# A fifth buffer of exponentials in an attention encoder, shared with the scaled rows of a part

## The chip, the cores and the metric

The kernel runs on one NeuronCore of one Trainium2 chip. The metric is the device time of one execution in microseconds (us): the median of three runs. Profiled times are counted from the start of the profiled span. The engines are called TensorE (PE), VectorE (DVE), ScalarE (ACT), GpSimd (POOL) and SyncE (SP, which only starts transfers).

## The reference

Four graph layers over N = 2708 nodes with 512 features, each followed by a residual and a layer norm. Only layer 0 is touched, and of it only the encoder. There, H = 4 heads of D = 128 features are weighted by a masked softmax over the adjacency matrix:

```python
Xw = einsum('hnd,hde->hne', Xh, W)
f1 = einsum('hnd,hd->hn', Xw, V[:, 0, :, 0])
f2 = einsum('hnd,hd->hn', Xw, V[:, 1, :, 0])
sig = sigmoid(f1[:, :, None] + f2[:, None, :])
local_att = masked_softmax(adj * sig, adj != 0)      # att is the mean of two equal ones
Xa = einsum('hij,hjd->hid', att, Xw)                  # encoder
Xn = batchnorm(Xa as N x 512)
...                                                   # an MLP block, then the decoder
Y = einsum('hij,hjd->hid', att, Yh)                   # the same att once more
```

So for each head a 2708 x 2708 matrix of exponentials is formed and multiplied with Xw; the sums of its rows divide the result. The decoder, the MLP and layers 1 to 3 follow.

## The kernel before, in words

**Parts and places.** The encoder is the first call of `attention_pass` (`first` is true). The 2708 destination nodes are cut into two halves of 1354 (`HSPAN`), the four heads into two pairs (`HP` = 2). Half by pair gives four parts, in this order: A1 (first half, first pair), B1 (first half, second pair), A2 and B2. In a part the 22 blocks of source nodes are taken in the order of `ORDER`; the position in it is called a place, 0 to 21. Place 11 is the last block, with only 20 nodes.

**One place.** `form` makes the exponentials of one block for both heads in one tile `t` of 128 x 2708 numbers: two tanh on ACT (L403, one for each head; the sigmoid written through tanh), one `scalar_tensor_tensor` on DVE (L411, "the masking step" below, for both heads), one exp on ACT (L412). In the A parts the adjacency block itself is prepared before, by two DVE steps (L391, L392), and stored for later passes; the B parts load the prepared block. PE then multiplies: `node_sums` issues for each head 11 products (10 of 128 destination nodes and one of 74), L433, that add up over the 22 places in four PSUM tiles for each head. Three of these tiles (tags po0 to po2) have a bank for each of the two heads; two more tiles hold the fourth bank of each.

**Buffers.** The tiles `t` come from a pool with four buffers (L479), so a tanh that writes a new tile waits until the tile four places before has been read by everything. The readers of a tile are PE and, in some places, a transfer on POOL's queue (L493, `kept`) that saves it in DRAM for the decoder: at places 8, 11, 14 and 18 in A parts and at places 1, 4, 7, 9, 11, 14, 17 and 20 in B parts (`KEPT`).

**The end of a part.** `keep` empties the eight banks on DVE: for each group of banks the sums are clamped (L634), inverted (L635) and multiplied with the results (L636) into the tile `rows` of that head (L623, a tag of its own with two buffers: one tile for each head). Each bank has to be emptied before the next part's first products can write it. Then `turn` transposes `rows` on PE (L653, 11 for each head, and one more for the sums, L661) into banks of the second head, and DVE copies these into `ft` (L673) and takes their statistics (L675). `turn` of the first head is called at place 0 of the next part, after the first head's products, and `turn` of the second head at place 1. The second head's products of places 0 and 1 come after that. The scaled tile of the row sums also goes to DRAM for the decoder.

**f1b.** Each part needs two tiles with the values of f1 of its heads, spread over the partitions, from three buffers. The first is loaded by SP ahead of time; the second (L464, started from ACT's queue) takes the buffer that the old part's first-head tanh of place 21 reads last.

**What sets the order.** A tile framework orders the instructions of each engine when the program is built, and each engine then runs its own list strictly in that list's order, waiting on semaphores. Which buffer a tile gets follows the order in which the tiles are asked for, the oldest one first. So a change in the buffers also changes the built lists. In the built list of ACT before, in A parts, the first-head tanh of a place stands directly ahead of the exp of two places before; in B parts ACT works in pairs of places.

Of the kernel before, what the change touches and what calls it, by code (L numbers as in the profile page):

```python
# [8 lines left out]
F32 = mybir.dt.float32  # L9
# [8 lines left out]
P = 128  # L18
# [11 lines left out]
def gnn_stack_kernel(  # L30
# [107 lines left out]
    NHALF, HB, HP = 2, 3, 2  # L138
    HW = 2 * ((N + 3) // 4)
# [12 lines left out]
    NB = len(NODES[0])  # L152
# [31 lines left out]
    with ExitStack() as l0:  # L184
# [143 lines left out]
        def spread_sums(att, hf, p):  # L328
# [6 lines left out]
                )  # L335
            return t

        def attention_pass(values, first, att, psum, finish, f1b=None, blocks=(), spread=None, rest=None, taken={}):


# [106 lines left out]
            for hf, (h0, w) in enumerate(HSPAN):  # L447
                for p in range(H // HP):
# [24 lines left out]
                    for place, jt in enumerate(ORDER):  # L473
                        n = BLOCKS[jt][1]


                        if place > (3 if first else 0) and later:
                            later.pop(0)()
                        t = att.tile([P, HP, HW], F32, tag="t", name="t", bufs=4)  # L479
                        tv = t[:n, :, :w]  # L480
                        kept = kept_d.get((hf, p, jt))
                        if kept is None or first:
                            rows = n if n == P else HR
                            with ExitStack() as order:

                                for ins in taken.values() if place == 2 else ():
                                    order.enter_context(tc.issue_after(ins.ins))
                                step = form(hf, p, jt, att, prepare, f1b, t[:rows, :, :w])
                            if rest is not None:
                                rest(step)  # L490
                                rest = None
                            if kept is not None:
                                nc.gpsimd.dma_start(kept[:n, :, :w], tv)  # L493
                        else:
                            for r in range(0, P if n == P else HB * Q, P if n == P else Q):
                                nc.sync.dma_start(t[r : r + n, :, :w], kept[:n, :, :w])
                            if p == 0 and jt in KEPT[1]:
                                count(hf, jt, att)
                        if po is None:


                            both = [
                                psum.tile([P, HP, BANK], F32, tag=f"po{q}", name="po", bufs=1)
                                for q in range(HB)
                            ]
                            po = [both[q][:, k, :] for k in range(HP) for q in range(HB)]
                            if first:
                                more = [
                                    psum.tile([P, BANK], F32, tag=f"psm{k}", name="po", bufs=1)
                                    for k in range(HP)  # L510
                                ]
                                po = [
                                    [both[q][:, k, :] for q in range(HB)] + [more[k]]
                                    for k in range(HP)
                                ]
                        if first:
                            node_sums(0, place, jt, t, w, hf)
                            waiting.append(lambda a=(1, place, jt, t, w, hf): node_sums(*a))
                            if turns:
                                turns.pop(0)()  # L520
                            if not turns:
                                for work in waiting:
                                    work()
                                waiting = []
                            continue
                        for k in range(HP):
                            h = HP * p + k
                            for q, (q0, qw) in enumerate(HCH[hf]):
                                r = 0 if n == P else q * Q
                                nc.tensor.matmul(  # L530
                                    po[HB * k + q][:, :qw],
                                    values[r : r + n, jt, h * P : (h + 1) * P],
                                    t[r : r + n, k, q0 : q0 + qw],
                                    start=(place == 0),
                                    stop=(place == NT - 1),
                                )
# [69 lines left out]
        with (  # L606
# [8 lines left out]
            def keep(hf, p, po, later):  # L615
                h0, w = HSPAN[hf]
                if hf == 0 and p == 0:
                    mlp_w.append(load_mlp(enc_wT, "enc_w"))
                kept = []
                for k in range(HP):  # L620
                    rc = att.tile([P, NB], F32, tag="rc", name="rc", bufs=4)
                    nc.vector.memset(rc[:, NB - 1 :], 1.0)
                    rows = att.tile([P, NB, P], F32, tag="rows", name="rows")  # L623
                    groups = []
                    for b in range(HB + 1):
                        own = list(range(b * PER, min(NB, (b + 1) * PER)))
                        whole = [r for r in own if NODES[hf][r][1] == P]
                        groups += [(b, g) for g in (whole, [r for r in own if r not in whole]) if g]
                    for b, g in groups:
                        m = NODES[hf][g[0]][1]  # L630
                        src = po[k][b][:m, g[0] % PER * DR : (g[-1] % PER + 1) * DR]
                        src = src.rearrange("p (r e) -> p r e", e=DR)
                        own = rc[:m, g[0] : g[-1] + 1]
                        nc.vector.tensor_scalar(own, src[:, :, P], TINY, None, ALU.max)  # L634
                        nc.vector.reciprocal(own, own)  # L635
                        taken[k] = nc.vector.tensor_tensor(  # L636
                            rows[:m, g[0] : g[-1] + 1, :],
                            src[:, :, :P],
                            own.unsqueeze(2).to_broadcast([m, len(g), P]),
                            ALU.mult,  # L640
                        )
                    kept.append((rows, rc))

                def turn(k):

                    h = HP * p + k
                    rows, rc = kept[k]
                    for b in range(TURNS):
                        slots = range(b * QUAD, min(NB, (b + 1) * QUAD))
                        bank = po[1][(TURNS * k + b) % (HB + 1)]  # L650
                        for r in slots:
                            i0, m = NODES[hf][r]
                            nc.tensor.transpose(  # L653
                                bank[:, r % QUAD * P : r % QUAD * P + m],
                                rows[:m, r, :],
                                ident[:m, :m],
                            )
                        c0 = b * BANK
                        cw = min(w, c0 + BANK) - c0
                        if b + 1 == TURNS:  # L660
                            nc.tensor.transpose(bank[:NB, BANK - P :], rc, ident)  # L661
                            sm = att.tile([NB, P], F32, tag="sm", name="sm")
                            nc.vector.tensor_copy(sm, bank[:NB, BANK - P :])
                            full = (NB - 1) * P
                            nc.gpsimd.dma_start(
                                rs_d[h, h0 : h0 + full].rearrange("(r i) -> r i", i=P),
                                sm[: NB - 1],
                            )
                            nc.gpsimd.dma_start(
                                rs_d[h : h + 1, h0 + full : h0 + w], sm[NB - 1 :, : w - full]  # L670
                            )
                        dst = ft[:, h, h0 + c0 : h0 + c0 + cw]
                        nc.vector.tensor_copy(dst, bank[:, :cw])  # L673
                        later.append(
                            lambda dst=dst, n=TURNS * hf + b: nc.vector.bn_stats(  # L675
                                stats[:, h, n, :], dst
                            )
                        )

                return [lambda k=k: turn(k) for k in range(HP)]  # L680
# [1380 lines left out]
```

## Time and profile before

| what | value |
|---|---|
| median of 3 runs | 3207.96 us (3207.13 to 3212.84) |
| the profiled execution | 3204.93 us, of which the span is 3203.1 us |
| encoder pass, first to last L433 on PE | 39.0 to 543.5 us |
| PE busy in it, by part (ends at 168.05, 290.70, 424.00, 543.50) | 114.7, 113.4, 117.6, 110.1 us |
| length of the parts | 129.05, 122.65, 133.30, 119.50 us |
| DVE busy by part | 116.1, 81.7, 124.1, 74.4 us |
| ACT busy by part | 110.0, 111.4, 110.3, 102.3 us |

The parts are cut where PE ends the products of place 21. Busy times of matmuls overlap a little, so PE's share is somewhat high. A line of the timeline has the start, the length, the engine, the line of the kernel and the operation, output and inputs, the shape and how many instructions were merged; in brackets stands how long the engine had been idle before and what ended the wait. PE's records come two for each product, so 44 records are one place of two heads.

### The profile page before, as it was taken

Reading aid. Unit: us, or ns where it says so; the run is one execution under the profiler, and the core shown is the slowest. Engines: PE = TensorE matmul, PEld = TensorE weight load, DVE = VectorE, ACT = ScalarE, POOL = GpSimd, SP = SyncE. Lnnn points to the kernel's source line nnn. Section 1 sums busy time; section 2 is a strip of 40 time slices with the busy share of each in tenths; the row PEclk is TensorE's granted clock in tenths of the full one; section 3 lists DMA queues with packets and bytes.
Section 4 is the critical chain, followed back from the end, with each engine's and each line's share of the span. In section 5 each row is a group of like instructions: output and inputs, shape, how many; then the busy total and the mean of one; then the engine's idle time right before and its main releaser. Section 6 shows DMA issues by size and latency. Waiting matters only on the chain.

```text
span 3203.1 us, 39602 instructions
## 1 busy us (share of the span) xinstructions
PE 3107.7 (97%) x15176; PEld 2353.6 (73%) x15176; DVE 2052.1 (64%) x3797; ACT 1350.0 (42%) x1615; POOL 203.6 (6%) x304
## 2 busy tenths in 40 slices
PE   8888899999999999999999999999999999999999
PEld 7888888454444446885578787777668888888886
DVE  7867975777587585445157766777644555555565
ACT  6898887567777552001133333434401111111111
POOL 1100100000000000000011111110110000000000
PEclk9999999999999999999999999999999999999999
DMA  7866764336545512551054444555431111111111
GB/s 278 297 206 218 280 244 158 109 122 254 177 160 200 184 61 84 144 134 47 30 152 128 148 147 145 157 172 176 133 107 36 49 51 51 49 49 53 49 44 34
DMA packets 203635, 425.81 MB, mean 133 GB/s; under 512 B 20798, under 2 KB 134562, under 8 KB 197622
## 3 DMA queue, kind: packets, MB, share of 16 engines
q1 hardware_dynamic: 179454, 319.92, 33.0%
q0 software_dynamic: 23552, 101.26, 8.4%
q8 instruction: 119, 1.95, 0.2%
q10 hardware_dynamic: 440, 2.10, 0.2%
q14 instruction: 70, 0.57, 0.1%
HBM read 325.88 MB, written 95.87 MB: 132 GB/s over the span
## 4 chain that ended last, share of the span: by engine, by line
PE 72%; issue 11%; DVE 7%; DMA 5%; ACT 3%; POOL 1%; SPq 0%; DVEq 0%; POOLq 0%; ACTq 0%
PE po L1537 18%; PE ps_s L1333 17%; PE po L530 10%; PE ps_nb L1147 7%; PE ps_wide L1197 5%; PE ps_hid L131 2%; PE ps_sup L1725 2%; PE ps_mlp L783 2%; PE po L433 2%; PE ps_dec L914 2%; PE ps_v L131 1%; ACT t L412 1%; DVE t L411 1%; ACT t L403 1%; DMA kept<-t 1%
## 5 line engine op out<-in xcount | busy, mean ns | idle before, releaser
L411 DVE SCALAR_TENSOR_TENSOR t<-t,a 128x2708 f32<-128x2708 f32 (+1 forms) x152 | 450.8, 2976 | 194.8 <-ACT t L403 189.7
L433 PE MATMUL po<-xw,t 128*128 128x129 f32 (+2 forms) x3872 | 448.5, 282 | 48.7 <-ACT t L412 39.0
L433 PEld LDWEIGHTS po<-xw,t 128*128 128x128 f32 (+2 forms) x3872 | 438.1, 192 | 59.2 <-ACT t L412 50.1
L403 ACT ACTIVATE t<-f1b,f2h 128x1354 f32<-128x1354 f32 (+1 forms) x304 | 415.3, 1412 | 74.6 <-PE po L530 33.1
L412 ACT ACTIVATE t<-t 128x2708 f32<-128x2708 f32 (+1 forms) x152 | 371.3, 2452 | 85.5 <-DVE t L411 85.1
L1333 PE MATMUL ps_s<-q,hT 128*128 128x256 f32 (+1 forms) x1848 | 405.5, 372 | 0.0
L530 PE MATMUL po<-t,emb 128*128 128x452 f32 (+3 forms) x1056 | 397.7, 545 | 3.9 <-ACT t L412 3.7
L1537 PE MATMUL po<-sup,e 128*128 128x256 f32 (+1 forms) x1512 | 397.3, 384 | 3.1 <-DVE c L1618 2.1
L1333 PEld LDWEIGHTS ps_s<-q,hT 128*128 128x128 f32 x1848 | 339.2, 190 | 49.8 <-issue 6.0
L530 PEld LDWEIGHTS po<-t,emb 128*128 128x128 f32 (+1 forms) x1056 | 193.5, 190 | 201.1 <-issue 190.8
L1537 PEld LDWEIGHTS po<-sup,e 128*128 128x128 f32 (+1 forms) x1512 | 264.3, 185 | 59.1 <-issue 21.9
L1537 PE MATMUL po<-held,T 128*128 128x256 f32 x1200 | 294.5, 380 | 4.7 <-DVE T L1494 4.7
L1537 PEld LDWEIGHTS po<-held,T 128*128 128x128 f32 x1200 | 226.4, 190 | 38.5 <-DVE T L1494 7.1
L1913 DVE SCALAR_TENSOR_TENSOR e<-a_cols,ps_s 128x512 f32<-128x512 f32 (+1 forms) x121 | 80.0, 661 | 237.9 <-PE ps_s L1333 232.0
L1333 PE MATMUL ps_s<-hT 128*128 128x256 f32 (+2 forms) x968 | 213.9, 372 | 3.4 <-DVE e L1823 2.4
L1333 PEld LDWEIGHTS ps_s<-hT 128*128 128x128 f32 x968 | 174.2, 190 | 30.6 <-issue 3.1
L1819 ACT ACTIVATE a_score<-a_score,neg_big 128x512 f32<-128x512 f32 (+2 forms) x131 | 88.8, 686 | 253.5 <-DMA a_score<-in_adjT_dram 109.5
L1147 PE MATMUL ps_nb<-hid_hi,at 128*128 128x512 f32 x484 | 185.6, 390 | 0.4 <-DVE at L1139 0.4
L1147 PE MATMUL ps_nb<-hid_lo,at 128*128 128x512 f32 x462 | 180.1, 390 | 0.0
L1443 ACT ACTIVATE e<-e 128x512 f32<-128x512 f32 (+1 forms) x187 | 113.5, 617 | 131.4 <-DVE e L1442 131.1
L1494 DVE TENSOR_TENSOR T<-e 128x256 f32<-128x256 f32 x200 | 84.5, 423 | 122.1 <-PE po L1537 98.3
L1905 ACT ACTIVATE q<-ps_wide,uq 128x256 f32<-128x256 f32 (+1 forms) x44 | 20.5, 466 | 336.9 <-PE ps_wide L1197 336.9
(275 smaller groups left out, 3945.7 us busy)
## 6 DMA issues: line engine op xcount, KB each, us to landing
a<-adj_d SPq DMA_DIRECT2D x108, 677.0 KB
a_cols<-in_adjT_dram SPq DMA_DIRECT2D x200, 256.0 KB
a<-in_adjT_dram SPq DMA_DIRECT2D x42, 677.0 KB
adj_d<-a POOLq DMA_DIRECT2D x42, 677.0 KB, 5.8
kept<-t POOLq DMA_DIRECT2D x20, 1354.0 KB, 7.3
t<-kept SPq DMA_DIRECT2D x20, 1354.0 KB
raw<-in_adjT_dram SPq DMA_DIRECT2D x105, 256.0 KB
a_score<-in_adjT_dram SPq DMA_DIRECT2D x55, 256.0 KB
```

What stands on the lines that cost most here:

```text
L131: nc.tensor.matmul(ps[:n], xt[:, c, :n], w[:, c, :], start=(c == 0), stop=(c == C - 1))
L403: tanh = nc.scalar.activation(tv[:, k, :], f1b[k][:n, :w], AF.Tanh, bias=f2h[:n, jt, h : h + 1], scale=0.5,)
L411: step = nc.vector.scalar_tensor_tensor(tv, tv, GUARD, ab, ALU.add, ALU.mult)
L412: exp = nc.scalar.activation(tv, tv, AF.Exp, scale=0.5)
L433: nc.tensor.matmul(po[k][b][:m, s * DR : (s + 1) * DR], t[own : own + n, k, i0 : i0 + m], values[own : own + n, jt, HP * pair + k, :], sta ...
L530: nc.tensor.matmul(po[HB * k + q][:, :qw], values[r : r + n, jt, h * P : (h + 1) * P], t[r : r + n, k, q0 : q0 + qw], start=(place == 0), ...
L1147: nc.tensor.matmul(pos[it][:n], at, half[:, jt, :], start=(jt == 0 and k == 0), stop=(jt == NT - 1),)
L1197: nc.tensor.matmul(ps[:, :width], w(c, o), xt(c), start=(c == 0), stop=(c == C - 1),)
L1333: nc.tensor.matmul(ps[:, jb, i:w], keys[:, c, j : j + P], st["q"][:, c, i:], start=(c == 0), stop=(c == C - 1),)
L1443: nc.scalar.activation(e, e, AF.Exp)
L1537: nc.tensor.matmul(po[bank][rows, half, :], lhsT, rhs, start=(k == 0 and half == 0) if first is None else first, stop=last, skip_group_che ...
L1819: nc.scalar.activation(a, a, AF.Identity, bias=neg_big[: a.shape[0]], scale=1.0e30)
```

## The change

A tile of exponentials in the encoder is now cut out of a slightly larger tile (128 x 2816 instead of 128 x 2708 numbers) of the same tag, which has five buffers. The scaled rows of both heads of a part, 2 x 11 x 128 numbers, are one such tile too, instead of two tiles with a tag of their own. So five buffers hold exponentials, and one of the five holds the scaled rows from the moment a part ends until they have been transposed. The decoder's pass keeps its own four buffers.

```diff
+        def wide_tile(att, name):
+            return att.tile([P, HP * NB * P], F32, tag="t", name=name, bufs=5)
+
...
-                        t = att.tile([P, HP, HW], F32, tag="t", name="t", bufs=4)
+                        if first:
+                            t = wide_tile(att, "t")[:, : HP * HW].rearrange(
+                                "p (k w) -> p k w", k=HP
+                            )
+                        else:
+                            t = att.tile([P, HP, HW], F32, tag="t", name="t", bufs=4)
...
                 kept = []
+                all_rows = wide_tile(att, "rows").rearrange("p (k r d) -> p k r d", k=HP, d=P)
                 for k in range(HP):
                     rc = att.tile([P, NB], F32, tag="rc", name="rc", bufs=4)
                     nc.vector.memset(rc[:, NB - 1 :], 1.0)
-                    rows = att.tile([P, NB, P], F32, tag="rows", name="rows")
+                    rows = all_rows[:, k]
```

Lines after the change are 3 to 9 higher: L403, L411, L412, L433, L634, L636 and L673 become L406, L414, L415, L436, L643, L645 and L682.

## The prediction

> **What bounds the kernel now.** I first read the costliest groups (line, engine, operation, count | busy, mean ns | idle ahead of them and what ended it):
>
> ```profile
> L411 DVE SCALAR_TENSOR_TENSOR t<-t,a 128x2708 f32<-128x2708 f32 (+1 forms) x152 | 450.8, 2976 | 194.8 <-ACT t L403 189.7
> L433 PE MATMUL po<-xw,t 128*128 128x129 f32 (+2 forms) x3872 | 448.5, 282 | 48.7 <-ACT t L412 39.0
> L412 ACT ACTIVATE t<-t 128x2708 f32<-128x2708 f32 (+1 forms) x152 | 371.3, 2452 | 85.5 <-DVE t L411 85.1
> ```
>
> The idle time of L433 is what matters: 48.7 us in the encoder, 39.0 of it for the exp. The other idle times say little, since by stage the bound differs. A place costs PE 39.41/8 = 4.93 us (eight unbroken places from 179.46, below). It costs ACT 4.98 in B parts (two places from 191.00 to 200.96) and DVE 5.49 in A parts (103.65 to 109.14: L391 0.86, L392 1.57, L411 2.98, small gaps). So A parts are bound by DVE; in B parts ACT and PE are level. Next the waits of ACT inside the encoder (total us, times, longest):
>
> ```profile
> ACT t L403 <- DMA kept<-t: 25.2, 9, 5.7
> ACT t L412 <- DVE t L411: 25.0, 16, 6.2
> ACT t L403 <- PE po L433: 10.5, 11, 2.6
> ```
>
> The `kept` transfers hold buffers, and a tanh waits. ACT's timeline in A1 shows how that reaches PE:
>
> ```profile
> 87.23 2.46 ACT L412 ACTIVATE t<-t 128x2708 f32<-128x2708 f32 x1 [0.18 <-DVE t L411]
> 95.44 1.43 ACT L403 ACTIVATE t<-f1b,f2h 128x1354 f32<-128x1354 f32 x1 [5.74 <-DMA kept<-t]
> 96.77 2.44 ACT L412 ACTIVATE t<-t 128x2708 f32<-128x2708 f32 x1
> ```
>
> The exp of place 10 (96.77) had its input at 92.69, but stood behind the tanh of place 12, which waited for place 8's transfer. PE then idled 4.35 us. Last, PE's timeline around A1's end and in B1:
>
> ```profile
> 162.87 5.62 PE L433 MATMUL po<-xw,t 128*128 128x129 f32 x48 [1.88 <-ACT t L412]
> 169.45 0.94 PE L433 MATMUL po<-xw,t 128*128 128x129 f32 x6 [0.97 <-DVE rows L636]
> ...
> 173.61 0.94 PE L433 MATMUL po<-xw,t 128*128 128x129 f32 x6 [1.67 <-DVE rows L636]
> ...
> 175.63 2.72 PE L433 MATMUL po<-xw,t 128*128 128x129 f32 x22 [0.69 <-ACT t L412]
> ...
> 179.46 39.41 PE L433 MATMUL po<-xw,t 128*128 128x129 f32 x352
> 221.02 1.16 PE L433 MATMUL po<-xw,t 128*128 128x129 f32 x8 [2.14 <-ACT t L412]
> ```
>
> and DVE's there:
>
> ```profile
> 170.07 0.13 DVE L634 TENSOR_SCALAR rc<-po 128x1 f32<-128x1 f32 x1
> 170.12 2.97 DVE L411 SCALAR_TENSOR_TENSOR t<-t,a 128x2708 f32<-128x2708 f32 x1
> 173.00 0.55 DVE L636 TENSOR_TENSOR rows<-po,rc 128x384 f32<-128x384 f32 x1
> ```
>
> PE ended place 21 at 168.04 and lost only 0.97 + 1.67 + 0.69 = 3.33 us there, since the masking step of B1's place 0 (160.50 to 163.48) and its exp were done before the emptying. The step at 170.12 is place 1's.
>
> **What the skill says.** "TensorE: Matmul & The Clock Gate", section "Architectural detail: the array is 16× 32×32, not 1× 128×128", says that ACT's and DVE's queues are strictly first in, first out. The trace agrees: the exp above sat 4.1 us behind a waiting tanh. The same page, "What's actually happening", has PE's clock fall to half after an idle window of about 3.4 us, the windows running freely. The trace agrees in kind: from 135.3 to 138.7 the granted clock was 0.51, after only 2.09 us of idleness, and 0.99 in the next 3.4 us. "Perfetto Trace Analysis", "Optimization Strategy", says that regular bubbles can mean that there is no room for a next tile. Only part of the bubbles here are of that kind, as the next steps show.
>
> **The change, step by step.** No instruction comes, goes or changes its size. What changes is which tile waits for which, and with it the built lists of the encoder. All sums are against the profiled execution, 3204.93 us (span 3203.1 and 1.8 around it), 3.0 below the median of 3207.96.
>
> (1) A parts, kept waits: 0. With five buffers a tanh of place p needs place p−5's buffer. But the built list also moves tanh one place ahead: place 13's now stands ahead of the exp of place 10, where place 12's stood. 13−5 = 8 as 12−4 = 8: the exp waits for the same transfer. So PE's gaps in A1 (4.35, 1.51, 2.09) and A2 (3.03, 1.51, 2.42) stay.
>
> (2) B parts, kept waits: −12.0. From place 7 on ACT's list has the old order, so each tanh needs a buffer one place older, now that of a place without a transfer or one finished a place longer. PE's gaps for the exp in B1 (2.14, 0.80, 0.74, 2.22 = 5.90) and B2 (2.96, 2.32, 0.78 = 6.06) go.
>
> (3) Ends of A1 and A2: −2.8. In the list before, the exp of place 21 stands behind the new part's second-head tanh, which waited 3.84 us for f1b. Now all three last exps stand ahead of the new part's six tanh. PE's gaps of 1.88 (at 162.87) and 0.90 (at 418.79) go, and no more, as PE had place 20 to do until 160.99.
>
> (4) A1 to B1 and A2 to B2: +7.2 each, +14.4. The scaled rows need a wide buffer, and the new part's place 0 gets a later place in DVE's list: its masking step moves behind the emptying, to where place 1's stood, and places 1 and 2 move back in turn. By the lines above that position comes 170.12 − 168.04 = 2.08 us after PE's end. Then masking 2.97, exp 2.46 and some 0.1 of hand-over: PE idles 7.6 us where it lost 0.97. Place 1's second-head products then wait for the transposed banks to be copied (L673), with the first head's copies queued behind place 2's masking step and the second head's behind place 3's: I take 1.4 + 1.6 us, estimates, being half a masking step each, with both ends 0 and 3.0. Together 10.6 for 3.33. What was hidden under PE's place 21 is thus uncovered.
>
> (5) B1 to A2: +2.5. The same move; PE started 3.58 us after its end at 290.70, now 7.6: +4.0. A2 is bound by DVE, which loses the 2.98 us that it used to spend on the masking step under PE's tail. If DVE has waits later to swallow it, +1; at most +4.
>
> (6) PE's clock: 0, between −3 and +5. Cold windows of 3.4 us cost PE half of their length, 1.7. Those at 234.3 and 275.3 follow gaps that go; three bubbles of 7.6 us bring up to three, of which B1 to A2 already has one (295.8 to 299.2).
>
> (7) The rest: 0. `ft`, the stored sums, the second pass's loads and the MLP keep their order; the 108 more numbers per tile are never touched.
>
> Sum: −12.0 − 2.8 + 14.4 + 2.5 = +2.1, so 3207.0 for a profiled execution and 3210 for the median.
>
> **Rivals.**
> (a) The bubble stays hidden: 3193. If PE loses no more at the boundaries than before, (4) and (5) vanish and −14.8 remains. For it: five buffers of exponentials, so tanh can be done early. Against it: tanh is not late there, the masking step's place in DVE's list is. It decides if PE's idleness after place 21 is under 3.3 us. Should the kept waits of A parts vanish too, 4.35 + 2.09 + 3.03 + 2.42 = 11.9 more would go; the built list speaks against that.
> (b) The gaps in B parts come back as a shortage at ACT: 3222. ACT's place, 4.98, is not shorter than PE's 4.93, so ACT can't build a lead in a B part; it lives from what it has at the start. After step (4) I estimate, from these rates and the new list, the exp of place 9 some 53 us and PE's need of it some 55 us after the first masking step: a margin of about 2 us. If waits for buffers or for DVE's `ft` copies use it up, PE waits per place again and (2) is lost: +2.1 + 12.0 = +14.
> (c) No effect beyond noise: the likeliest case. The gains of (2) and (3), 14.8, and the losses of (4) and (5), 16.9, are of one size, each uncertain by 3 to 4: −4 to +8 around 3208, thus 3204 to 3216.
>
> **How the numbers follow.** Likeliest case 0.57, (a) 0.15, (b) 0.28. A measurement of this kernel can tell about 0.2%, 6.4 us, from no change. Of the likeliest case 0.52 lie within that and 0.05 above; (b) is mostly above, (a) below. Faster 0.15, same 0.53, slower 0.32. The range reaches into (a) and up to (b): 3197 to 3222. The likeliest alone has 3204 to 3216, its centre being 3210.
>
> **What the profile after would show.** (1) right: ACT's wait for `kept` of 5 to 6 us near 95 is still there. (2): no PE gap over 0.5 us for the exp between the tenth place of B1 and its end. (3): no gap of 1.9 us ahead of place 21. (4), (5): three PE gaps of about 7.6 us for the exp after 166, 288 and 415 or so, with place 0's masking step on DVE in the midst of the emptying. (6): the number of windows at half clock in the encoder, nine before. The prediction is wrong if these gaps are near 3, or if B parts again show gaps of 2 us for the exp.

## The result, and the profile after

The changed kernel takes 3198.3 us (median of 10 runs, 3193.77 to 3204.67); the kernel before, run beside it, 3207.92 (10 runs). The ratio is 0.9971, 95% interval 0.9960 to 0.9982: faster by 0.29%, where +2 us was forecast. The profiled executions are closer: spans of 3196.2 and 3203.1. One execution of either kernel can lie 4 us and more from its median, so what follows compares parts of the encoder, and not spans.

The groups after the change, columns as before:

```profile
L436 PE MATMUL po<-xw,t 128*128 128x129 f32 (+2 forms) x3872 | 444.2, 281 | 43.7 <-ACT t L415 42.6
L415 ACT ACTIVATE t<-t 128x2708 f32<-128x2708 f32 (+1 forms) x152 | 371.7, 2453 | 96.7 <-DVE t L414 96.3
```

PE's idle time in the products fell from 48.7 to 43.7 us only; but 42.6 of it now comes from the exp. The waits of ACT in the encoder:

```profile
ACT t L415 <- DVE t L414: 36.2, 24, 3.8
...
ACT t L406 <- DMA kept<-t: 11.8, 6, 3.2
ACT t L406 <- PE po L662: 5.8, 3, 2.4
ACT t L406 <- PE po L436: 2.5, 2, 1.8
```

The waits for saved tiles fell from 25.2 to 11.8 us, and those for PE's products from 10.5 to 2.5. New are 5.8 us of waits for the transposes (L662), which let go of the shared buffer. Of the 11.8 us all but 1.2, at the end of B1, are in A parts. ACT's timeline in A1:

```profile
94.14 1.42 ACT L406 ACTIVATE t<-f1b,f2h 128x1354 f32<-128x1354 f32 x1 [2.35 <-DMA kept<-t]
95.47 2.44 ACT L415 ACTIVATE t<-t 128x2708 f32<-128x2708 f32 x1
```

This is the exp of place 10 again, behind a tanh (now of place 13) that waits for place 8's transfer, as the prediction had it. PE's timeline, from A1 to the start of A2:

```profile
97.97 10.40 PE L436 MATMUL po<-xw,t 128*128 128x129 f32 x88 [3.58 <-ACT t L415]
...
132.06 29.86 PE L436 MATMUL po<-xw,t 128*128 128x129 f32 x264 [0.64 <-ACT t L415]
169.50 5.10 PE L436 MATMUL po<-xw,t 128*128 128x129 f32 x22 [7.59 <-ACT t L415]
174.40 1.88 PE L662 MATMUL po<-ident,rows 128*128 128x128 f32 x11
...
176.33 2.69 PE L436 MATMUL po<-xw,t 128*128 128x129 f32 x22
...
267.07 14.99 PE L436 MATMUL po<-xw,t 128*128 128x129 f32 x132 [0.60 <-ACT t L415]
289.65 5.10 PE L436 MATMUL po<-xw,t 128*128 128x129 f32 x22 [7.59 <-ACT t L415]
```

and DVE's behind A1's end at 161.91:

```profile
163.94 0.13 DVE L643 TENSOR_SCALAR rc<-po 128x1 f32<-128x1 f32 x1
163.99 2.97 DVE L414 SCALAR_TENSOR_TENSOR t<-t,a 128x2708 f32<-128x2708 f32 x1
166.88 0.55 DVE L645 TENSOR_TENSOR rows<-po,rc 128x384 f32<-128x384 f32 x1
...
171.07 2.97 DVE L414 SCALAR_TENSOR_TENSOR t<-t,a 128x2708 f32<-128x2708 f32 x1
175.49 1.29 DVE L682 COPY ft<-po 128x512 f32<-128x512 f32 x2 [1.46 <-PE po L662]
...
177.90 2.95 DVE L414 SCALAR_TENSOR_TENSOR t<-t,a 128x2708 f32<-128x2708 f32 x1
180.78 1.27 DVE L682 COPY ft<-po 128x512 f32<-128x512 f32 x2
```

So the bubble is there: the masking step begins 2.08 us after PE's end, and with masking and exp PE idles 7.59 us at each of the three boundaries (the third ends at 422.54). The wait that was forecast behind it, for the copies (L682), is not: after 169.50 PE works without a gap until 266. In B1 one gap of 0.60 for the exp is left where there were four of 5.90 in all; in B2 none.

**An account by part.** I cut the encoder as before and split each part's length, from the records of PE and the granted clock in the trace: idle (no matmul of any kind runs), lost to the clock (half of PE's busy time while half the clock was granted), and the rest. Each part is from one execution. The differences after minus before in us; each part holds the boundary at its start:

| part | forecast | length | idle | clock | rest |
|---|---|---|---|---|---|
| A1 | −1.9 | −5.64 (128.99 to 123.35) | −4.10 | −1.44 | −0.10 |
| B1 | +1.3 | −2.53 (122.67 to 120.14) | −1.05 | −0.40 | −1.08 |
| A2 | +1.6 | −0.36 (133.26 to 132.89) | +1.87 | −2.38 | +0.15 |
| B2 | +1.1 | −0.18 (119.48 to 119.30) | −1.77 | +2.79 | −1.20 |
| sum | +2.1 | −8.71 | −5.05 | −1.43 | −2.23 |

The encoder began 0.5 earlier too, and the work behind it took 2.2 longer in this execution; that work took 2657 to 2664 us in the profiles of this study, without an order among the kernels.

### The profile page after: what moved, and what is told of

Its sections match the earlier page's. It is cut to its first block, busy times and chain, and to the rows that moved or that the text cites. A ratio compares the mean times of both kernels' runs of the same rounds, so it can differ in the third digit from the quotient of the medians.

```text
span 3196.2 us, 39584 instructions
## 1 busy us (share of the span) xinstructions
PE 3104.5 (97%) x15176; PEld 2353.4 (74%) x15176; DVE 2050.9 (64%) x3797; ACT 1349.7 (42%) x1615; POOL 204.0 (6%) x304
## 4 chain that ended last, share of the span: by engine, by line
PE 76%; DVE 8%; issue 6%; ACT 5%; DMA 4%; POOL 1%; SPq 0%; DVEq 0%; POOLq 0%; ACTq 0%
PE po L1546 18%; PE ps_s L1342 17%; PE po L538 10%; PE ps_nb L1156 7%; PE po L436 6%; PE ps_wide L1206 5%; PE ps_sup L1734 2%; PE ps_mlp L792 2%; PE ps_hid L131 2%; ACT t L415 2%; ACT t L406 2%; PE ps_dec L923 2%; DVE t L414 2%; PE ps_v L131 1%; DVE e L1832 1%
## 5 line engine op out<-in xcount | busy, mean ns | idle before, releaser
L414 DVE SCALAR_TENSOR_TENSOR t<-t,a 128x2708 f32<-128x2708 f32 (+1 forms) x152 | 450.6, 2975 | 171.0 <-ACT t L406 165.4
L436 PE MATMUL po<-xw,t 128*128 128x129 f32 (+2 forms) x3872 | 444.2, 281 | 43.7 <-ACT t L415 42.6
L436 PEld LDWEIGHTS po<-xw,t 128*128 128x128 f32 (+2 forms) x3872 | 435.4, 192 | 52.0 <-ACT t L415 48.0
L406 ACT ACTIVATE t<-f1b,f2h 128x1354 f32<-128x1354 f32 (+1 forms) x304 | 414.3, 1412 | 55.0 <-PE po L538 33.2
L415 ACT ACTIVATE t<-t 128x2708 f32<-128x2708 f32 (+1 forms) x152 | 371.7, 2453 | 96.7 <-DVE t L414 96.3
L1452 ACT ACTIVATE e<-e 128x512 f32<-128x512 f32 (+1 forms) x187 | 113.5, 617 | 133.5 <-DVE e L1451 133.1
```

Source lines behind the costliest of these rows:

```text
L406: tanh = nc.scalar.activation(tv[:, k, :], f1b[k][:n, :w], AF.Tanh, bias=f2h[:n, jt, h : h + 1], scale=0.5,)
L414: step = nc.vector.scalar_tensor_tensor(tv, tv, GUARD, ab, ALU.add, ALU.mult)
L415: exp = nc.scalar.activation(tv, tv, AF.Exp, scale=0.5)
L436: nc.tensor.matmul(po[k][b][:m, s * DR : (s + 1) * DR], t[own : own + n, k, i0 : i0 + m], values[own : own + n, jt, HP * pair + k, :], sta ...
L1452: nc.scalar.activation(e, e, AF.Exp)
```

## The experiments

My theory after the result: the fifth buffer wins what was forecast in B parts, and the boundaries lose by the bubble; but behind the bubble I had added a wait that isn't there. After the first four experiments (shared4, warm, early1, early2) I added that in A parts I had counted gaps of PE where only the end of DVE's work counts. The rival: the gain comes from the new order of the lists, and the buffer has little to do with it. Ratios are to the kernel before, timed in five rounds beside each.

**shared4: the sharing without the fifth buffer.**

```diff
-            return att.tile([P, HP * NB * P], F32, tag="t", name=name, bufs=5)
+            return att.tile([P, HP * NB * P], F32, tag="t", name=name, bufs=4)
```

> The changed kernel with four wide buffers in place of five: the scaled rows are still shared. Theory: the sharing costs at the boundaries (bubbles of 7.6 us stay), and all of the gain is the fifth buffer's; without it the waits for saved tiles in B parts are back with their cold clock (9.3 + 6.9 us) and some in A parts: 3216 (3210 to 3224), slower than both kernels. Rival: the gain comes from the new order of the lists and not from the buffer: 3198 to 3203.

Measured: 3217.0, ratio 1.0031 (1.0019 to 1.0043). B1 took 131.0 and B2 127.4, against 120.1 and 119.3 with five. In its waits of ACT,

```profile
ACT t L406 <- DMA kept<-t: 27.2, 10, 5.5
```

the saved tiles are back. For the whole and for B parts the theory stands: there the gain is the buffer's, and the sharing alone is a loss. For A1 it does not: with four buffers A1 took 125.4, which is 3.6 of the 5.6 us that the changed kernel gained there. In A1 the rival, the new order of the lists, seems to have most of the gain: place 21's exp no longer stands behind the wait for f1b. exp_first below, with four buffers too, agrees.

**hold_b and hold_a: the saved tiles let go early, in the kernel before.** Both leave out most of what is saved for the decoder and put other numbers there. hold_b does it in B parts, as shown; hold_a has `p == 0` and does it in A parts.

```diff
-                                nc.gpsimd.dma_start(kept[:n, :, :w], tv)
+                                if p == 1:
+                                    cut = w // 16
+                                    nc.gpsimd.dma_start(kept[:n, :, :cut], tv[:, :, :cut])
+                                    fill = xw[:n, : 2 * ((w - cut) // 512 + 1)].rearrange(
+                                        "p (k j) h e -> p k (j h e)", k=HP
+                                    )
+                                    nc.gpsimd.dma_start(
+                                        kept[:n, :, cut:w], fill[:, :, : w - cut]
+                                    )
+                                else:
+                                    nc.gpsimd.dma_start(kept[:n, :, :w], tv)
```

> The kernel before (four buffers), but in B parts a saved tile is cut: one sixteenth of it is saved from the tile itself, the rest of the same bytes comes from the resident values, so that the buffer is free when the small transfer has landed; the decoder then works on other numbers for these blocks. Theory: the waits for saved tiles in B parts cost their gaps and the half clock behind them, so B1 goes from 122.7 to about 113.4 and B2 from 119.5 to about 112.6: 3192 (3188 to 3196). As the prediction priced it, gaps alone: B1 116.8, B2 113.4, 3197. Rival: the tanh waits for PE anyway: 3208.

> The kernel before with the same cut in A parts (places 8, 11, 14, 18) and B parts untouched; again other numbers reach the decoder. Theory: DVE's masking steps set the end of A parts and stand still for a saved tile only once (1.6 us before place 18 of A1), so that A1 gets shorter by 2 to 4 us and A2 by 0 to 2: 3204 (3201 to 3207). Rival, the prediction's own count of gaps of PE: 11.9 us and three or four cold windows of 1.7: 3190 to 3196.

Measured: hold_b 3201.9, ratio 0.9986 (0.9980 to 0.9993); hold_a 3199.6, 0.9974 (0.9963 to 0.9984). Both built lists also moved work of the prologue, so that the first product came at 44.5 and 44.9 us and not at 39.0; the totals can't be used, the parts can. hold_b: B1 116.65 and B2 116.53 (−6.0 and −3.0), with one gap of 2.3 left in each; 113.4 and 112.6 were expected with the clock, 116.8 and 113.4 by the gaps alone. By the same account B1 has 3.6 us less idleness and 1.7 less lost to the clock, B2 3.7 less idleness and 1.6 more lost to the clock. So the saved tiles' waits do cost B parts time, and the prediction's count is the nearer, but neither is shown: a gap of 2.3 stayed, and half clock came with it (245.5 to 249.0, 494.7 to 498.1). hold_a: A1 −5.3 and A2 −2.2, but its list also puts two masking steps ahead of the emptying, and B1, where nothing was let go, changed by −5.7. How much of A1 the saved tiles hold is not told by it; for the changed kernel e0_back3 below tells.

**exp_first: place 21's exp ahead of the new part's tanh, in the kernel before.**

```diff
+                last_exp[0] = exp
...
                                 for ins in taken.values() if place == 2 else ():
                                     order.enter_context(tc.issue_after(ins.ins))
+                                if first and place == 0 and last_exp:
+                                    order.enter_context(tc.issue_after(last_exp[0].ins))
```

> The kernel before, but the next part's first tanh may not be issued before the exp of place 21, so that this exp no longer stands behind the wait for f1b. Theory: A1 shorter by 1.9 to 2.1 and A2 by 0.9 to 1.1, B parts within 1 us of before: 3205 (3203 to 3207). Rival: the tanh comes too late for the next part's place 0 now, and the boundary takes the gain back: 3208 to 3212.

Measured: 3205.6, ratio 0.9992 (0.9984 to 1.0001), no difference that can be told. A1 −3.8 and A2 −3.8, where 1.9 to 2.1 and 0.9 to 1.1 were expected; B1 +1.2 and B2 +3.5, where 1 at most was; the encoder −2.9. The gap ahead of place 21 goes in A1 (0.25 is left in A2). Behind it the emptying has changed its order too. The idleness at the two boundaries is about the old 3.3 us (3.3 and 3.8), but most of it is one wait, and the half clock follows it (167.2 to 170.6 and 419.8 to 426.6), which costs 1.7 and 2.6 us. Both views were half right.

**e0_back3: no exp behind a saved tile in A parts, in the changed kernel.** The one place that the list had moved ahead is taken back; on DVE and PE the order of the encoder's instructions stays. `exps` holds the exps in the order in which they are formed. (The forming of a place is also made a function, `begin`, of which early1 below has more.)

```diff
...
+                    if p == 0 and place >= 3:
+                        order.enter_context(tc.issue_after(exps[-3].ins))
```

> The changed kernel with one order added: in A parts the tanh of a place stands behind the exp of three places before, so that place 13's no longer stands ahead of place 10's exp. On DVE and PE nothing moves. Theory: the PE gaps for saved tiles in A parts go (3.58 and 0.64 in A1, 1.58 and the like in A2), but DVE's masking steps set the end of A parts: A1 from 123.35 to about 121.9, A2 within 0.5 of 132.9: 3197 (3195 to 3199). Rival, by the prediction's way of counting: all gaps and their cold windows count, 8 to 12 us: 3188.

Measured: 3196.8, ratio 0.9966 (0.9954 to 0.9978), not to be told from the changed kernel's. A1 121.94 and A2 132.88, as expected to 0.1. ACT's timeline of e0_back3 shows what changed:

```profile
93.52 2.46 ACT L415 ACTIVATE t<-t 128x2708 f32<-128x2708 f32 x1 [0.40 <-DVE t L414]
97.04 2.74 ACT L406 ACTIVATE t<-f1b,f2h 128x1354 f32<-128x1354 f32 x2 [1.06 <-DMA kept<-t]
```

The exp now runs as DVE hands over its tile, and the tanh waits behind it, which costs nothing. Yet in A2 nothing is gained: place 21's masking step comes when DVE has done the 21 before it, and 2.98 + 2.46 + 5.17 = 10.6 us after its start the part is over. These are place 21's masking steps in A1 and in A2, of the kernel before (L411), the changed kernel, and in A1 of e0_back3:

```profile
152.32 2.98 DVE L411 SCALAR_TENSOR_TENSOR t<-t,a 128x2708 f32<-128x2708 f32 x1
149.79 2.98 DVE L414 SCALAR_TENSOR_TENSOR t<-t,a 128x2708 f32<-128x2708 f32 x1
151.12 2.98 DVE L414 SCALAR_TENSOR_TENSOR t<-t,a 128x2708 f32<-128x2708 f32 x1
...
409.51 2.98 DVE L411 SCALAR_TENSOR_TENSOR t<-t,a 128x2708 f32<-128x2708 f32 x1
404.25 2.98 DVE L414 SCALAR_TENSOR_TENSOR t<-t,a 128x2708 f32<-128x2708 f32 x1
```

From the start of A1 (39.05, 38.56, 39.88) that is 113.3, 111.2 and 111.2 us. With 10.6 more, 121.9 is the floor that DVE sets, and e0_back3 is 0.1 above it. In A1 the changed kernel was 1.4 us above e0_back3, the kernel before 7.0. Gaps of PE that end before the floor don't count.

The other kernels with the changed kernel's list in A1 as far as place 16 show how far the waits for saved tiles scatter between executions: PE's two gaps at places 10 and 16 were 3.58 and 0.64 there, 4.82 and 1.91 in early1, 3.78 and 0 in early2, 5.21 and 1.06 in warm (below); with four buffers 4.35 and 2.09 before, 4.11 and 2.14 in shared4, 2.50 and 3.17 in exp_first. Some of what the table shows for A1 is this scatter. At place 10 no gain of the fifth buffer shows, as the prediction had it; at place 16 the gaps with five buffers are all below those with four.

**warm and e0_warm: PE kept busy in the bubble.** The added products go to an emptied bank, and the next part overwrites them.

```diff
+                if (hf, p) != (len(HSPAN) - 1, H // HP - 1):
+                    for _ in range(28):
+                        nc.tensor.matmul(
+                            po[0][HB][:, :DR], ident, xw[:, 0, 0, :], start=True, stop=True
+                        )
```

> The changed kernel with 28 products more at each of the three boundaries (6.2 us of work for PE at full clock), into a bank that is already emptied and that the next part overwrites. They fill the bubble and bring nothing else. Theory: the half clock after a bubble costs by itself (10.2 us at half clock from 167 to 177, of them 6.4 with PE busy): at each boundary the first places of the next part get 2 to 3 us shorter, 3192 (3189 to 3196). Rival: behind a bubble PE waits for the copies and masking steps anyway, so that its clock does not matter: 3198, or a little more if the added products delay it.

> e0_back3 with the 28 products at each boundary of warm. There the A parts, whose saved tiles no longer hold an exp up, end at DVE's pace in both, so that the added work shows in the B parts alone. Theory: the half clock behind a bubble costs 2 to 3 us at each change from an A to a B part, and nothing at B1 to A2, where DVE is late anyway: A1 121.9, B1 117.3, A2 132.9, B2 117.2, 3192 (3190 to 3195). Rival: it costs nothing, B1 119.9 and B2 119.2, 3197.

Measured: warm 3192.8, ratio 0.9959 (0.9943 to 0.9974); e0_warm 3187.4, 0.9937 (0.9923 to 0.9950). e0_warm against e0_back3: A1 121.94 and 121.94, B1 117.31 for 119.94, A2 134.32 for 132.88, B2 117.31 for 119.19. The total is below its range (3190 to 3195), the parts are as expected but for A2. In B parts 2.6 and 1.9 us at a boundary are the half clock's. The added products also changed the lists of DVE and ACT there, but PE's first product comes 7.6 us behind the boundary in both kernels and PE waits little after it, so the lists can't be the gain. A2, where nothing was expected, lost 1.4: there the half clock only came later (0.50 from 294.7 to 297.5, behind a wait of 2.88 us for the copies), the second head's transposes ended later, and DVE waited 1.7 us for them where it had waited 0.2. The encoder gains 3.1. The medians differ by more; of the 7.1 us between the two profiled executions 4.3 lie behind the encoder, where the kernels are alike, and these runs don't explain them. The stretches of the changed kernel behind the bubble (busy time of the engines, then the granted clock, DMA share and GB/s),

```profile
166.70:170.10 3.40, 0.60 (x3) 0.60 (x3) 3.40 (x4) 2.46 (x1) 0.00 (x0) 0.50 0.62 199
170.10:173.50 3.40, 3.40 (x17) 3.40 (x17) 3.33 (x6) 3.10 (x2) 0.34 (x1) 0.50 0.61 201
```

and those of e0_warm:

```profile
166.70:170.10 3.40, 2.06 (x18) 1.87 (x18) 3.40 (x4) 2.46 (x1) 0.00 (x0) 1.00 0.56 172
170.10:173.50 3.40, 3.40 (x33) 3.40 (x32) 3.33 (x6) 2.91 (x2) 0.15 (x1) 1.00 0.65 201
```

33 records of matmuls for 17 in the same 3.4 us. PE's timeline of e0_warm shows the bubble filled, and what is left of the wait for the copies:

```profile
161.93 6.42 PE L675 MATMUL po<-xw,ident 128*128 128x129 f32 x56
169.69 2.72 PE L437 MATMUL po<-xw,t 128*128 128x129 f32 x22 [1.34 <-ACT t L415]
...
174.88 2.28 PE L437 MATMUL po<-xw,t 128*128 128x129 f32 x18 [0.76 <-DVE ft L708]
```

At full clock that wait is 0.76 us, not 3.0.

**early1 and early2: the next part's first places ask for their buffers ahead of the scaled rows.** The forming of a place becomes a function `begin`; e0_back3 has it too, and there DVE's and PE's order in the encoder is the changed kernel's. early1's calls are shown; early2 has 2 in place of the 1.

```diff
                     if first:
+                        nhf, npr = (hf, p + 1) if p + 1 < H // HP else (hf + 1, 0)
+                        for q in range(1 if nhf < len(HSPAN) else 0):
+                            begun[nhf, npr, q] = begin(nhf, npr, q)
                         turns = finish(hf, p, po, later)
```

> The changed kernel, but the first two places of the next part ask for their buffers (and are traced) before the part's scaled rows do; nothing else. Theory: the three bubbles of 7.6 us come only from the order in which buffers are asked for, which puts place 0's masking step behind the emptying. Then the bubbles shrink to about 1 us or less, the cold clock after them goes too, and the boundaries give back 6.8 + 3.4 + 6.7 us and some of the 3.3 that the kernel before lost at two of them: 3180 (3175 to 3186), B parts as short as in the changed kernel. Rival: the bubble only moves, since ACT and DVE then owe the same work later (B parts live from the lead that they have at the start): about as the changed kernel, 3198.

> As early2, but only place 0 of the next part asks before the scaled rows. Theory: the boundaries of the kernel before come back (masking step of place 1 in the midst of the emptying, PE losing about 3.3 us there), with the five buffers in between: 3184 (3179 to 3190), some 3 to 4 us behind early2. Rival as there: 3198.

Measured: early1 3193.7, ratio 0.9957 (0.9941 to 0.9974); early2 3194.4, 0.9961 (0.9947 to 0.9976). Both are above their ranges (3179 to 3190 and 3175 to 3186), nearer to the rival's 3198. The bubbles are gone, B1 and B2 take 114.8 and 114.3 (early1), 113.2 and 113.0 (early2); but A1 and A2 take 127.7 and 135.5, and 129.2 and 139.4. So the bubble does come from the order in which the buffers are asked for, but the rest of the forecast failed. In early2 the new part's first masking step and its exp stand ahead of place 21's on DVE and ACT, and PE idles 3.95 us ahead of place 21; in both the waits for saved tiles of A1 (above) are still there.

**e1_all, e1_back3, e2_back3: early1 and early2 with the order of e0_back3.** e1_all has, besides, exp_first's order.

> early1 with two orders added: the next part's first tanh behind the exp of place 21, and in A parts the tanh of a place behind the exp of three places before, so that no exp stands behind a wait for a saved tile. Theory: early1 has short B parts (114.8 and 114.3) but gave 4.3 and 2.6 us back in A parts, to the f1b wait and to the kept waits of place 8 and 14; with these gone A1 comes to 122, A2 to 131 to 132 (bound by DVE), B parts stay: 3186 (3182 to 3190), faster than both kernels. Rival: A parts are bound by DVE at 5.49 us a place, and what early1 lost there was the masking step moved into them: 3192 to 3194 as early1.

> early1 with the same order in A parts, and nothing on the new part's tanh. Theory: B parts as in early1 (114.8 and 114.3), A1 near 122 as in e1_all, A2 near 133.5: the encoder at 485 (against 492.3 in early1, 495.7 in the changed kernel): 3188 (3185 to 3191), faster than both kernels. Rival: what A parts gain, the boundary takes back, because the new place 0's masking step now waits behind place 21's exp: 3193 to 3196 as e1_all.

> early2 with the same order in A parts. Theory: B parts as in early2 (113.2 and 113.0), A1 and A2 shorter than its 129.2 and 139.4 by the kept waits, but still with the f1b wait or the two masking steps ahead of the emptying: 3188 to 3192. Rival: DVE carries two masking steps more in A parts, so nothing is won on early2: 3194.

Measured:

| kernel | us | ratio | A1 | B1 | A2 | B2 |
|---|---|---|---|---|---|---|
| e1_all | 3195.4 | 0.9962 (0.9949 to 0.9974) | 121.9 | 118.2 | 133.5 | 119.0 |
| e1_back3 | 3183.7 | 0.9927 (0.9913 to 0.9941) | 122.0 | 114.8 | 131.5 | 115.6 |
| e2_back3 | 3187.5 | 0.9938 (0.9925 to 0.9950) | 126.6 | 111.5 | 134.1 | 111.3 |

e1_back3 has the lowest time of the study, faster than both kernels by an interval that doesn't meet the changed kernel's, and below its own range (3185 to 3191); the intervals of e2_back3, e0_warm and the two kernels below overlap with it. e2_back3 gained on early2, against its rival, and came in just under its 3188 to 3192. e1_back3's PE timeline at the end of A1:

```profile
156.12 5.62 PE L437 MATMUL po<-xw,t 128*128 128x129 f32 x48 [0.32 <-ACT t L415]
162.71 0.94 PE L437 MATMUL po<-xw,t 128*128 128x129 f32 x6 [0.97 <-DVE rows L666]
166.86 0.94 PE L437 MATMUL po<-xw,t 128*128 128x129 f32 x6 [1.67 <-DVE rows L666]
```

The boundary is that of the kernel before (0.97 and 1.67), with 0.32 lost ahead of place 21. In e1_all the theory fell (3182 to 3190 was expected): A1 came to 121.9 as it said, but its exp order makes place 0's tanh and so its masking step late, DVE begins the emptying behind it, and PE waits 3.71 us for the emptying. Its rival's number (3192 to 3194) was nearer, but for another reason; the rival of exp_first had named this one.

**e2_mask and e1_mask: on DVE, place 0 behind place 21's masking step.**

`steps` holds the masking steps in the order in which they are formed.

```diff
...
+                    if place == 0 and steps:
+                        order.enter_context(tc.issue_after(steps[-1].ins))
```

> e2_back3 with one order more: on DVE the next part's place 0 stands behind the masking step of place 21. In early2 and e2_back3 it stood ahead of it, place 21 came a masking step late, and PE idled 3.95 and 3.54 us ahead of place 21. Theory: that was the whole of what early2 lost in A parts; now A1 comes to DVE's floor of 121.9 or up to 1 us above it, B1 and B2 stay at 111.4, A2 at 131 or less: 3178 (3174 to 3183). Rival: the two masking steps must be done somewhere ahead of the emptying, and the time lost only moves to the boundary: 3185 to 3188, as e2_back3.

> The same order added to e1_back3, where at the ends of A1 and A2 the place 0 already stood behind place 21: only the end of B1 changes. Theory: within 2 us of e1_back3, 3184 (3182 to 3187). Rival: at the end of B1 the earlier masking step was of use, and A2 gets longer by up to 3 us: 3187.

Measured: e2_mask 3186.4, ratio 0.9933 (0.9920 to 0.9946); e1_mask 3185.0, 0.9929 (0.9914 to 0.9943). e2_mask is no better than e2_back3: A1 128.9, A2 134.0, with 4.39 us of PE's idleness ahead of place 21. The rival stands, and ACT's timeline of e2_mask shows where the time went:

```profile
153.08 4.05 ACT L406 ACTIVATE t<-f1b,f2h 128x1354 f32<-128x1354 f32 x3 [3.16 <-DMA f1b<-f_d]
157.04 7.14 ACT L415 ACTIVATE t<-t 128x2708 f32<-128x2708 f32 x3
```

Place 21's exp (157.04) is now behind the tanh of two new places and their wait for f1b. With f1b's second tile loaded into the buffer that place 21's tanh frees, two places ahead come too soon by about that wait. A fourth buffer for f1b might take that wait away; it was not tried. e1_mask's time is as e1_back3's, as expected; but in its profiled execution A2 took 134.8 for 131.5 and B2 114.3 for 115.6. For A2 its rival was right: the earlier masking step at the end of B1 was of use.

## Why the prediction was wrong

The time lies at the low end of the stated range (3197 to 3222), but the sign was not forecast: +2.1 for −8.7 us in the encoder. Of the 10.8 us between them, idleness is 7.2, the clock 1.4 and the rest 2.2. By the steps of the prediction:

(4), the boundaries into B1 and B2, is the step that failed most. The bubble was right to 0.01 us (7.59 for 7.6). The 1.4 + 1.6 us of waits for the copies, added at each of the two boundaries, were not there: 0 in the changed kernel, 0.76 at full clock in e0_warm. The prediction had named 0 as one end of these estimates, and added the middle. By the timelines of DVE and PE above, the first head's copies (175.49) were not held up by place 2's masking step (171.07 to 174.04): PE, at half clock, did the transposes only from 174.40 to 176.28, and DVE had waited 1.46 us for the first of them. At full clock, in e0_warm, they were held up (from 171.26 the masking step, from 174.14 the copies), and that is the 0.76. The second head's copies did come behind place 3's masking step, at 180.78 as forecast, but PE had other products in its list and went on from 180.13. So the step costs 4.3 us of idleness at a boundary, where the prediction took 7.2; with the two corrected, the forecast would have been −3.9.

(1), that A parts gain nothing, failed in its size. The mechanism is in the trace (place 10's exp behind place 13's tanh, which waited 2.35 us, not 5 to 6), but the gaps came out 2.2 us smaller in A1, in part by the scatter of the transfers; in A2 they sum to 7.1 for 7.0. And the count was of the wrong thing: an A part can't end before the start of DVE's last masking step and 10.6 us more, and e0_back3 shows A1 ending at that floor, at 121.94. The kernel before was 7.0 us above it, so that much was there to be had, and the changed kernel took 5.6 of it. How these divide between (1) and (3) is not shown: shared4 and exp_first, which have (3)'s order with four buffers, took 3.6 and 3.8 us from A1, where (3) was priced at 1.9, and each is one execution.

(6), the clock at 0, was right as a sum (−1.4, within −3 to +5), but by luck: by part it was −1.4, −0.4, −2.4 and +2.8. Each bubble brought 10.2 us at half clock, three stretches of 3.4 us where one was reckoned with, and the A parts lost fewer. Half clock came in nine stretches of the encoder before and in six after, but these are longer. In A2 step (5) was right: place 21's masking step began 3.4 us later in the part (122.2 us for 118.8) for +2.5. But the kernel before ended A2 3.8 us above DVE's floor, 0.9 of it by the gap that f1b made, and the changed kernel 0.1 above it, with 2.4 us less lost to the clock.

What no step priced is the rest, −2.2. A stretch of matmuls ends with a record of 0.27 us, while within it one comes every 0.112; so each interruption counts some 0.16 us more as busy. B1 had seven gaps before and has two now: five times 0.16 is 0.8 of its 1.08. That is an estimate from these records; no run tested it.

(2) was right, and so was (3) for the gaps. Of B1's and B2's gaps of 12.0 us 0.6 is left, and shared4 brings them back (7.7 and 5.5); the gaps of 1.88 and 0.90 ahead of place 21 are gone.

Of the rivals, (a), a hidden bubble, gave the nearer number (3193), but for a reason that the trace refutes; (b), a shortage at ACT, shows at most as the one gap of 0.60. In (c) the balance of gains and losses was taken too even, by the 6 us of (4).

## What to carry to other kernels

When a pool rotates, a tile that is asked for early and written late can hold up the later tiles of its tag in the built lists, as the scaled rows did here: ask for the tiles that can be filled first, and price such a move by the place that the step gets in its engine's list. Before a gap is counted as a gain or a loss, find the engine whose own chain sets the end of that stage; gaps of another engine ahead of it can be free, as in A2. And when a wait is added behind a bubble, look at what the waiting engine still has to do and when it will get there: here 3.0 of the 7.2 us priced did not come.

## What the hardware showed beyond what was expected

PE's clock fell after idleness much shorter than the half-clock stretch that it brought. In the kernel before, a gap of 2.09 us was followed by 3.4 us at 0.51, and in early1 one of 1.91 us by 3.4 us at 0.50; but a gap of 2.14 us (ended at 221.02) was followed by none, so the length of a gap alone doesn't tell. A bubble of 7.59 us brought 10.2 us at half clock, 5.3 to 6.0 of them with PE at work (the expectation of warm has 6.4), worth 2.6 and 1.9 us where PE was the bound (e0_warm). Filling a bubble with products that nobody needs was worth that much in itself in B parts, and cost 1.4 us in A2. And PE's gap at one place of the same list, behind the saving of one tile (1354 KB), differed by up to 1.9 us between executions.
